# Rounding the last chunk's intermediate rows in two halves, and placing unread TensorE products by the planner's own clock

## The chip, the core and the metric

The kernel runs on one core of one Trainium2 chip. A core has five engines that work side by side, each through its own instructions in order: TensorE (PE in the profile; PEld is its loading of weights), VectorE (DVE), ScalarE (ACT), GpSimd (POOL) and SyncE (SP), which here issues the transfers between memory and the on-chip buffers. The metric is the time of one execution on the device in microseconds (us). The kernel before takes 2631.14 us, the median of three runs (2631.13 to 2632.89).

## What is computed

The input `x` has 8 sequences of 1024 rows and 256 columns, in 32 bit. Four blocks follow each other, each added to its own input:

```
x = x + linear_attention_layer(layernorm(x))    # 16 heads of 16, running sums over the rows,
                                                # then norm, 256->1024 gelu ->256, norm
x = x + relu(layernorm(x) @ w1 + b1) @ w2 + b2  # 256->1024->256
x = x + softmax(Q K^T / 16) V                   # of layernorm(x), one head of 256
x = x + fp4_linear(silu(g) * u, w_down)         # g, u = fp4_linear(layernorm(x), w_gate / w_up)
```

The last block has 704 intermediate columns. `fp4_linear` rounds both of its operands, in blocks of 16 neighbouring columns, to a grid of eight sizes times a scale that is the block's largest size over 6. A block of 16 is rounded without looking at any other block, and 352 columns are 22 whole blocks.

## The kernel before, in words

**Tiling.** Rows are taken in chunks of 128 (8 in a sequence, 64 in all) and, in the first two blocks, in groups of 4 chunks (16 groups). A product on TensorE has 128 rows of weights and up to 512 columns; its result lies in one of 8 banks of PSUM. 32 bit products appear in the trace as two records, turns (transposes) as one.

**The stages.** `linear_group` and `linear_span` (lines 909 to 1125) make a group's normalized rows (`n`, `n0T`), its `k` and `q` (products of `n0T` with `wk` and `wq`), and a serial chain of running sums: sums on DVE (`prod`), a product with `hsum` on PE, a reciprocal and a product (`flow`) on DVE, spreading over the rows, sums again (`hsum` a second time), an exponential on ACT (`e`), a small product (`total,front`), and `scale`. The first group is cut into two spans, chunks 0 and 1 and chunks 2 and 3, and spreads `flow` and `scale` by products with `mask`; all other groups spread them through memory (two `packed` writes, then `spread` reads, on SP). `linear_chunk` (1127) does the attention of one chunk (`qz`, `sc`, `v_pad`, `kv_sum`, `wo`) and ends in `h`. `dense` (1331) makes the two wide blocks from halves of a group, with `w_in` and `w_out` streamed from memory through five buffers each; `norms_1` (1441) and `norms_2` (1462) stand behind its halves. `soft_chunk` (1502) makes softmax and the fp4 block of one chunk. The fp4 weights (`w_raw`) are rounded once, in the first 345 us, by `fp4_weights` (691).

**The end of a chunk.** `soft_chunk` makes `hid` (128 x 704) in two column halves: two products each for gate and up, `Silu` on ACT, a product on DVE. Then `fp4` (650) rounds all 704 columns at once: largest size, scale and reciprocal on DVE, a scaling, a square on ACT (`q_c`), four more DVE instructions. PE turns `hid` in six tiles, four into one bank and two into another; ACT copies each bank (`hqT`); six products with `wdT` give the row block, DVE adds `rows` to it (`y`), and SP writes it out.

**Who sets the order.** The order of all instructions is fixed when the kernel is built. Every stage is a Python generator that yields what its next step needs: an engine, tiles, banks, a condition (`when`) and a place in the order (`at`). `Plan.run` (291) always goes on with the part that can start first by the planner's own model of time. The model is in `Plan.took` (160): each call that is recorded by `Queue` (324, all its instructions carry line 337 in the profile) is given a start and a cost, and moves `free`, the time from which its engine is free, `done`, the time at which a tile is written, and `ran`, the time at which TensorE's last product ends. A product that starts over 2 us behind `ran` sets `slow`: up to then, products are costed at twice their length.

**Unread products.** Where the plan sees TensorE standing for more than 1.6 us ahead of its next step, `run` calls `fill` (1650), which puts in products of the identity matrix with itself, whose result nobody reads:

```
pause = max(now, best[2]) - self.ran
if pause > 1.6 and ...:
        self.fill(pause - 0.7)
```

`fill` takes 0.22 off that length for each product. The products go through `took` like all others, from `free["tensor"]` on, which may lie behind `ran`; `run` then sets `free` anew. `ident` is made by a helper outside the plan, so the plan has no time for it.

Of the kernel before, what the change touches and what calls it, by code (L numbers as in the profile page):

```python
# [22 lines left out]
INTER = 704  # L23
# [12 lines left out]
INTER_TILES = [(t * P, min(P, INTER - t * P)) for t in range((INTER + P - 1) // P)]  # L36
# [26 lines left out]
class Plan:  # L63
# [11 lines left out]

    def __init__(self, tc, nc):
        self.tc, self.nc = tc, nc
        self.free = {}
        self.done = {}
        self.by = {}  # L80
        self.banks = []
        self.live = {}
        self.slots = {}
        self.kind = {}
        self.size = {k: v[0] for k, v in TILES.items()}
        self.spare = False
        self.used = {}
        self.held = set()
        self.kept = set()
        self.last = {}  # L90
        self.act_set = 0
        self.landed = [0.0] * 8
        self.tiled = False
        self.ran = self.slow = 0.0
        self.fill = None
        self.parts = []
        for name in ("tensor", "vector", "scalar", "gpsimd", "sync"):
            setattr(self, name, Queue(self, name))
# [157 lines left out]
    def pe(self, *tiles, **kw):  # L256
        return self.need("tensor", tiles, **kw)

    def dve(self, *tiles, **kw):
        return self.need("vector", tiles, **kw)  # L260

    def act(self, *tiles, **kw):
        return self.need("scalar", tiles, **kw)
# [27 lines left out]
    def run(self):  # L291
        while self.parts:
            now = self.free.get("tensor", 0.0)
            best = None
            for part in self.parts:
                t = self.ready(part[1])
                if t is None:
                    continue
                stays = self.tiled and part[1].tiled
                queue = part[1].queue  # L300
                wait = max(max(t) - now - (0.3 if stays or part[2] < 0.0 else 0.0), 0.0)
                urgent = part[2] < 0.0
                unripe = 0.0 if urgent else max(t[1] + self.RIPE[queue] - now, 0.0)
                key = wait, unripe, queue == "tensor", not stays, part[2]
                if best is None or key < best[0]:
                    best = key, part, max(t)
            assert best is not None, "every part waits for another"
            pause = max(now, best[2]) - self.ran
            if pause > 1.6 and best[1][1].queue == "tensor" and self.fill is not None:
                if (self.banks_free(best[1][1].banks + 1) or 0.0) <= self.ran + 0.4:  # L310
                    self.fill(pause - 0.7)
            if best[0][0] > 0.0 or best[1][1].queue == "tensor":
                self.free["tensor"] = max(now, best[2])
            part = best[1]
            need = next(part[0], None)
            if need is None:
                self.parts.remove(part)
            else:
                part[1] = need
                if need.at is not None:  # L320
                    part[2] = need.at
# [34 lines left out]
def block_stack_kernel(ctx: ExitStack, tc: tile.TileContext, a: dict, out: bass.AP):  # L356
# [20 lines left out]
    plan = Plan(tc, tc.nc)  # L377
    nc, pe, dve, act, dma = plan, plan.pe, plan.dve, plan.act, plan.dma
    x_dram = a["L0_attn_inputs"]
    B, L, _ = x_dram.shape  # L380
    NCH = L // P
# [20 lines left out]
    def fresh(kind, need, name=None):  # L402

        need.fresh = kind
        yield need
        return make(kind, name)
# [49 lines left out]
    nc.gpsimd.iota(row_i, pattern=[[0, 1]], base=0, channel_multiplier=1)  # L456
    ident = const.tile([P, P], F32, name="ident")
    make_identity(tc.nc, ident)
    bdiag = const.tile([P, P], F32, name="bdiag")
    make_block_diagonal(tc.nc, bdiag, DH)  # L460
    triu = const.tile([P, P], F32, name="triu")
# [188 lines left out]
    def fp4(src, width, rows=P):  # L650

        nb = width // QB
        src = src[:rows, :width]  # L660
        amax = small([P, INTER // QB], "x_amax", 2)[:rows, :nb]
        nc.vector.tensor_reduce(
            amax, blocks(src, width), AX.X, ALU.max, apply_absolute_value=True
        )
        sc = small([P, INTER // QB], "x_s", 4)[:rows, :nb]
        nc.vector.tensor_scalar(sc, amax, 1.0 / 6.0, 1e-12, ALU.mult, ALU.max)
        rc = small([P, INTER // QB], "x_r", 3)[:rows, :nb]
        nc.vector.reciprocal(rc, sc)
        yield dve(rc)
        nc.vector.scalar_tensor_tensor(  # L670
            blocks(src, width),
            blocks(src, width),
            1.0 - 2.0**-23,
            wide(rc, rows, nb),
            ALU.mult,
            ALU.mult,
        )
        tile_c = yield from fresh("q_c", act(src))
        c = tile_c[:rows, :width]
        nc.scalar.activation(c, src, AF.Square, scale=(2.0**22 / 6.0) ** 0.5)  # L680
        yield dve(c)
        nc.vector.tensor_scalar(c, c, 2.0**22 * 4.0 / 3.0, None, ALU.add)
        nc.vector.tensor_tensor(src, src, c, ALU.add)
        yield dve(src)
        nc.vector.tensor_tensor(src, src, c, ALU.subtract)
        plan.drop(tile_c)
        nc.vector.tensor_tensor(
            blocks(src, width), blocks(src, width), wide(sc, rows, nb), ALU.mult
        )
# [812 lines left out]
    def soft_chunk(cc):  # L1502
# [2 lines left out]
        q = seqs[s]  # L1505
        n2T, vt = q["n2T"], q["vt"]
        at = 3.5 + min(cc, B * NCH - 10) / 4
        yield pe(
            banks=1,
            when=lambda: count["asked"] == cc  # L1510
            and count["asked"] - count["valued"] < (3 if plan.spare else 2),
        )
        bank = mm_bank()
        for e in range(2):
            for k in range(2):
                nc.tensor.matmul(
                    bank[:, e * P : (e + 1) * P],
                    lhsT=wqk[:, k, e * P : (e + 1) * P],
# [10 lines left out]
        banks = []  # L1529
        for kb in range(NG):  # L1530
            yield pe(qT, banks=1)
            bank = mm_bank()
            plan.keep(bank)
            for e in range(2):
                nc.tensor.matmul(
                    bank, lhsT=qT[:, e, :], rhs=n2T[kb][:, e, :], start=e == 0, stop=e == 1
# [9 lines left out]
        prob = []  # L1546
# [9 lines left out]
        for kb in range(NG):  # L1556
            yield pe(prob[kb], banks=1, at=at + 0.25)
            bank = turned([prob[kb][:, j * P : (j + 1) * P] for j in range(G)])
# [32 lines left out]
        for j0 in range(0, INTER, INTER // 2):  # L1591
            cols = slice(j0, j0 + INTER // 2)
            yield pe(xqT, banks=2)
            gb, ub = mm_bank()[:, : INTER // 2], mm_bank()[:, : INTER // 2]
            for bank, wT in ((gb, wgT), (ub, wuT)):
                for k in range(2):
                    nc.tensor.matmul(
                        bank,
                        lhsT=xqT[:, k, :],
                        rhs=wT[:, k, cols],  # L1600
                        start=k == 0,
                        stop=k == 1,
                    )
            if hid is None:
                hid = yield from fresh("hid", act(gb))
            else:
                yield act(gb)
            nc.scalar.activation(hid[:, cols], gb, AF.Silu)
            yield dve(hid)
            nc.vector.tensor_tensor(hid[:, cols], hid[:, cols], ub, ALU.mult)  # L1610
        plan.drop(xqT)
        yield dve(hid)
        yield from fp4(hid, INTER)
        hqT = []
        for half in range(2):
            yield pe(hid, banks=1, at=at + 0.75)
            tiles = INTER_TILES[4 * half : 4 * half + 4]
            bank = turned([hid[:, f0 : f0 + P] for f0, _ in tiles])
            hqT.append((yield from fresh("prob", act(bank), "hqT")))
            hqT[half] = hqT[half].rearrange("p (k t) -> p k t", k=4)  # L1620
            nc.scalar.copy(hqT[half][:, : len(tiles), :], bank)
        yield pe(*hqT, banks=1)
        bank = mm_bank()
        for k in range(len(INTER_TILES)):
            nc.tensor.matmul(
                bank[:, :D],
                lhsT=hqT[k // 4][:, k % 4, :],
                rhs=wdT[:, k, :],
                start=k == 0,
                stop=k == len(INTER_TILES) - 1,  # L1630
            )
# [6 lines left out]
        nc.sync.dma_start(out=out[s, c * P : (c + 1) * P, :], in_=y)  # L1638
        plan.drop(y)

    def softmax_and_fp4():
        for cc in range(B * NCH):
            q = seqs[cc // NCH]
            yield dve(
                at=3.5 + min(cc, B * NCH - 10) / 4,
                when=lambda: q["normed"] == NCH and cc - count["out"] < (8 if plan.spare else 4) and "softmax" in weights and "ends" in late,
            )
            plan.start(soft_chunk(cc), 3.5 + min(cc, B * NCH - 10) / 4)

    def fill(us):  # L1650

        bank = mm_bank()
        while us > 0.0:
            nc.tensor.matmul(bank[:, :P], lhsT=ident, rhs=ident, start=True, stop=True)
            us -= 0.22
        plan.let_go(bank)

    plan.fill = fill
# [45 lines left out]
```

## Time and profile before

| | |
|---|---|
| median of three runs | 2631.14 us |
| profiled execution | 2630.5 us |
| its span (first to last instruction) | 2628.6 us |
| PE busy | 2595.1 us |
| DVE busy | 1924.2 us |
| ACT busy | 1297.4 us |
| unread products (`bank<-ident`) | 94 products, 188 records, 24.0 us busy |
| first record on PE | 3.10 us |
| last product on PE starts, DVE's last `y` | 2622.56 us, 2625.45 us |

Times are counted from the first instruction. A row of the order of time has its start, its length, the engine, the line, the operation, output and inputs by their names in the program, shapes, the number of merged records, and in brackets the idle time of the engine ahead of it with what ended it. A row of busy time by stage has the stretch, its length, busy us (and records) of the engines in the order PE, PEld, DVE, ACT, POOL, then the granted clock of TensorE as a share of full speed, the busy share of the transfer engines and GB/s; where it was asked for one engine, it has that engine's busy time alone. A row of a group has the operation with its shapes and count, then busy us and mean ns of one, then idle time ahead of it with what ended it.

### The profile page before, as it was taken

How to read it: one execution, taken by the hardware profiler on the slowest of the kernel's cores; microseconds unless marked ns; L12 is line 12 of the kernel's file. 1: busy time of each engine (PE TensorE's matmuls, PEld its weight loads, DVE VectorE, ACT ScalarE, POOL GpSimd, SP SyncE). 2: the span in 40 equal slices, each digit the busy share in tenths (PEclk: the TensorE clock that was granted, in tenths of full speed). 3: DMA queues.
4: the chain of work that ended last, by engine and by line, in shares of the span. 5: the costliest groups of instructions: out<-in, count | busy, mean ns of one | idle time of the engine just before them, and what ended most of it. 6: DMA issues, size and time to landing. Idle time of an engine off the chain costs nothing.

```text
span 2628.6 us, 46432 instructions
## 1 busy us (share of the span) xinstructions
PE 2595.1 (99%) x16891; PEld 2031.8 (77%) x16891; DVE 1924.2 (73%) x4353; ACT 1297.4 (49%) x2665; POOL 577.7 (22%) x1101
## 2 busy tenths in 40 slices
PE   8989999999999999999999999999999999999999
PEld 7777777777777777787777777777787777877777
DVE  7888786868768587685867768686785877755687
ACT  4534445455364554636445364553645545354443
POOL 2333232222212122131221312122121221211000
PEclk9999999999999999999999999999999999999999
DMA  3425333223132232322323223232322312222000
GB/s 94 125 86 155 99 87 103 79 69 107 57 99 73 71 109 62 91 71 76 101 65 98 68 82 85 74 105 63 93 75 69 109 59 87 71 77 81 25 3 22
DMA packets 286819, 211.94 MB, mean 81 GB/s; under 512 B 24704, under 2 KB 275072, under 8 KB 286592
## 3 DMA queue, kind: packets, MB, share of 16 engines
q1 hardware_dynamic: 286592, 208.97, 27.7%
q8 instruction: 135, 2.21, 0.3%
q14 instruction: 92, 0.75, 0.1%
HBM read 188.17 MB, written 20.71 MB: 79 GB/s over the span
## 4 chain that ended last, share of the span: by engine, by line
PE 86%; DVE 8%; DMA 2%; ACT 2%; issue 1%; POOL 0%; SPq 0%; DVEq 0%; POOLq 0%; ACTq 0%
PE bank L337 86%; DVE prod L337 3%; DMA spread<-packed 2%; ACT L337 1%; DVE spread L337 1%; DMA packed<-flow 1%; DVE ln_st L337 0%; DVE u L337 0%; ACT prob L337 0%; DVE hid L337 0%; DVE r L337 0%; DVE res L337 0%; DVE w_raw L337 0%; ACT n0T L337 0%; DVE ln_mv L337 0%
## 5 line engine op out<-in xcount | busy, mean ns | idle before, releaser
L337 PE MATMUL bank<-half,w_in 128*128 128x256 f32 x2048 | 530.5, 382 | 3.6 <-DVE res L337 1.2
L337 PE MATMUL bank<-w_out,hidden 128*128 128x256 f32 x2048 | 532.2, 383 | 0.2 <-ACT hidden L337 0.2
L337 POOL TENSOR_SCALAR ln_ve<-ln_mv 128x1 f32<-128x1 f32 x384 | 97.7, 254 | 1691.8 <-DVE ln_mv L337 1672.4
L337 PEld LDWEIGHTS bank<-w_out,hidden 128*128 128x128 f32 x2048 | 369.5, 190 | 92.7 <-issue 39.7
L337 PEld LDWEIGHTS bank<-half,w_in 128*128 128x128 f32 x2048 | 380.2, 191 | 76.7 <-issue 26.6
L337 ACT ACT_TABLE_LOAD x322 | 413.1, 1283 | 7.9 <-DVE nmax L337 2.0
L337 ACT ACTIVATE hidden<-bank,c_L_ffn_b 128x256 f32<-128x256 f32 x256 | 121.7, 475 | 333.7 <-PE bank L337 333.6
L337 POOL TENSOR_TENSOR ln_rstd<-ln_ve,neghalf 128x1 f32<-128x1 f32 x384 | 238.0, 620 | 32.0
L337 PE MATMUL bank<-n2T,qT 128*128 128x512 f32 x512 | 241.7, 594 | 0.2 <-ACT qT L337 0.2
L337 PE MATMUL bank<-vt,probT 128*128 128x256 f32 x1024 | 231.5, 379 | 0.0
L337 PEld LDWEIGHTS bank<-vt,probT 128*128 128x128 f32 x1024 | 193.4, 190 | 28.3 <-issue 2.4
L337 ACT ACTIVATE hidden<-bank,c_L_attn_b 128x256 f32<-128x256 f32 x256 | 120.2, 470 | 187.0 <-PE bank L337 186.8
L337 PE MATMUL bank<-wdT,hqT 128*128 128x256 f32 x768 | 176.2, 379 | 0.5 <-ACT hqT L337 0.5
L337 PE MATMUL bank<-wgT,xqT 128*128 128x352 f32 x512 | 172.5, 459 | 0.0
L337 PE MATMUL bank<-wuT,xqT 128*128 128x352 f32 x512 | 172.3, 459 | 0.0
L337 DVE TENSOR_TENSOR hid<-hid,bank 128x352 f32<-128x352 f32 x116 | 59.9, 516 | 151.8 <-PE bank L337 124.2
L337 PEld LDWEIGHTS bank<-wdT,hqT 128*128 128x128 f32 x768 | 145.3, 190 | 20.9 <-ACT hqT L337 0.7
L337 DVE TENSOR_TENSOR sc<-bank,triu 128x512 f32<-128x512 f32 x240 | 148.7, 680 | 8.4 <-PE bank L337 7.7
L337 PEld LDWEIGHTS bank<-n2T,qT 128*128 128x128 f32 x512 | 92.8, 190 | 66.9 <-issue 59.8
L337 PEld LDWEIGHTS bank<-wuT,xqT 128*128 128x128 f32 x512 | 97.3, 190 | 54.2
L337 PEld LDWEIGHTS bank<-wgT,xqT 128*128 128x128 f32 x512 | 94.2, 190 | 32.9 <-issue 0.7
L337 DVE TENSOR_REDUCE mx<-bank 128x1 f32<-128x512 f32 x128 | 86.2, 674 | 35.0 <-PE bank L337 35.0
(220 smaller groups left out, 4401.6 us busy)
## 6 DMA issues: line engine op xcount, KB each, us to landing
w_in<-in_L_attn_W_dram SPq DMA_DIRECT2D x256, 128.0 KB
w_out<-in_L_attn_W_dram SPq DMA_DIRECT2D x256, 128.0 KB
w_in<-in_L_ffn_w_dram SPq DMA_DIRECT2D x256, 128.0 KB
w_out<-in_L_ffn_w_dram SPq DMA_DIRECT2D x256, 128.0 KB
spread<-packed SPq DMA_DIRECT2D x90, 256.0 KB
x<-in_L_attn_inputs_dram SPq DMA_DIRECT2D x64, 128.0 KB
xr<-in_L_attn_inputs_dram SPq DMA_DIRECT2D x64, 128.0 KB
rows<-res SPq DMA_DIRECT2D x64, 128.0 KB
```

What stands on the lines that cost most here:

```text
L337: ins = method(*args, **kw)
```

## The change

There are two edits.

In the planner, `fill` is no longer given a length but the time up to which products are wanted: 0.8 ahead of the step that TensorE waits for. It puts `free["tensor"]` back to `ran`, lets `took` place the products one by one, at the lengths that `took` gives them (twice as long while the model holds TensorE's clock to be slow), until that time is reached, and then restores `free`. The plan also knows from now on that `ident` is written by POOL at 3.0, and `free["tensor"]` begins at 0.0 explicitly. The order of all other instructions follows from the planner's model, in which `ran` and `slow` now differ.

In `soft_chunk`, the last chunk of all (`alone`) starts a part `half_rounded` for each column half of `hid` as soon as it is made, which rounds 352 columns by itself. PE then turns two tiles (columns 0 to 255, out of the first half) into the first bank and four into the second, ACT copies the banks, and the first two products with `wdT` need the first copy alone. All other chunks are as before.

```diff
@@ -75,7 +75,7 @@
 
     def __init__(self, tc, nc):
         self.tc, self.nc = tc, nc
-        self.free = {}
+        self.free = {"tensor": 0.0}
         self.done = {}
         self.by = {}
         self.banks = []
@@ -308,7 +308,7 @@
             pause = max(now, best[2]) - self.ran
             if pause > 1.6 and best[1][1].queue == "tensor" and self.fill is not None:
                 if (self.banks_free(best[1][1].banks + 1) or 0.0) <= self.ran + 0.4:
-                    self.fill(pause - 0.7)
+                    self.fill(max(now, best[2]) - 0.8)
             if best[0][0] > 0.0 or best[1][1].queue == "tensor":
                 self.free["tensor"] = max(now, best[2])
             part = best[1]
@@ -456,6 +456,7 @@
     nc.gpsimd.iota(row_i, pattern=[[0, 1]], base=0, channel_multiplier=1)
     ident = const.tile([P, P], F32, name="ident")
     make_identity(tc.nc, ident)
+    plan.done[ident.tensor.name], plan.by[ident.tensor.name] = 3.0, "gpsimd"
     bdiag = const.tile([P, P], F32, name="bdiag")
     make_block_diagonal(tc.nc, bdiag, DH)
     triu = const.tile([P, P], F32, name="triu")
@@ -1505,6 +1506,7 @@
         q = seqs[s]
         n2T, vt = q["n2T"], q["vt"]
         at = 3.5 + min(cc, B * NCH - 10) / 4
+        alone, rounded = cc >= B * NCH - 1, []
         yield pe(
             banks=1,
             when=lambda: count["asked"] == cc
@@ -1608,23 +1610,31 @@
             nc.scalar.activation(hid[:, cols], gb, AF.Silu)
             yield dve(hid)
             nc.vector.tensor_tensor(hid[:, cols], hid[:, cols], ub, ALU.mult)
+            if alone:
+                plan.start(half_rounded(hid, cols, rounded), at + 0.6)
         plan.drop(xqT)
-        yield dve(hid)
-        yield from fp4(hid, INTER)
+        if not alone:
+            yield dve(hid)
+            yield from fp4(hid, INTER)
         hqT = []
-        for half in range(2):
-            yield pe(hid, banks=1, at=at + 0.75)
-            tiles = INTER_TILES[4 * half : 4 * half + 4]
+
+        cut = 2 if alone else 4
+        for first, tiles in ((0, INTER_TILES[:cut]), (cut, INTER_TILES[cut:])):
+            yield pe(
+                hid, banks=1, at=at + 0.75, when=lambda: not alone or len(rounded) > bool(first)
+            )
             bank = turned([hid[:, f0 : f0 + P] for f0, _ in tiles])
-            hqT.append((yield from fresh("prob", act(bank), "hqT")))
-            hqT[half] = hqT[half].rearrange("p (k t) -> p k t", k=4)
-            nc.scalar.copy(hqT[half][:, : len(tiles), :], bank)
-        yield pe(*hqT, banks=1)
+            t = (yield from fresh("prob", act(bank), "hqT")).rearrange("p (k t) -> p k t", k=4)
+            nc.scalar.copy(t[:, : len(tiles), :], bank)
+            hqT.append(t)
+        yield pe(*(hqT[:1] if alone else hqT), banks=1)
         bank = mm_bank()
         for k in range(len(INTER_TILES)):
+            if alone and k == cut:
+                yield pe(hqT[1])
             nc.tensor.matmul(
                 bank[:, :D],
-                lhsT=hqT[k // 4][:, k % 4, :],
+                lhsT=hqT[k // cut if k < cut else 1][:, k % cut if k < cut else k - cut, :],
                 rhs=wdT[:, k, :],
                 start=k == 0,
                 stop=k == len(INTER_TILES) - 1,
@@ -1638,6 +1648,13 @@
         nc.sync.dma_start(out=out[s, c * P : (c + 1) * P, :], in_=y)
         plan.drop(y)
 
+    def half_rounded(hid, cols, rounded):
+
+
+        yield dve(hid)
+        yield from fp4(hid[:, cols], INTER // 2)
+        rounded.append(cols)
+
     def softmax_and_fp4():
         for cc in range(B * NCH):
             q = seqs[cc // NCH]
@@ -1647,12 +1664,13 @@
             )
             plan.start(soft_chunk(cc), 3.5 + min(cc, B * NCH - 10) / 4)
 
-    def fill(us):
+    def fill(until):
 
         bank = mm_bank()
-        while us > 0.0:
+        now, plan.free["tensor"] = plan.free["tensor"], plan.ran
+        while plan.free["tensor"] < until:
             nc.tensor.matmul(bank[:, :P], lhsT=ident, rhs=ident, start=True, stop=True)
-            us -= 0.22
+        plan.free["tensor"] = now
         plan.let_go(bank)
 
     plan.fill = fill
```

## The prediction

> **What bounds the kernel now.** I read the page first, then busy time by stage, then the order of events where TensorE is not full. Span and shares:
>
> ```profile
> span 2628.6 us, 46432 instructions
> ...
> PE 2595.1 (99%) x16891; PEld 2031.8 (77%) x16891; DVE 1924.2 (73%) x4353; ACT 1297.4 (49%) x2665; POOL 577.7 (22%) x1101
> ```
>
> PE is the bound, so the end moves only by what PE loses: idle time, products that nobody reads (they count as busy), and time at half clock. Busy time by stage (window, length, then each engine, granted clock, DMA share, GB/s):
>
> ```profile
> 0.00:60.31 60.31, 51.13 (x480) 43.88 (x480) 42.87 (x113) 23.99 (x64) 13.63 (x38) 1.00 0.37 97
> 60.31:161.41 101.10, 92.39 (x627) 72.84 (x627) 82.08 (x200) 47.24 (x118) 28.89 (x53) 0.97 0.40 114
> 161.41:340.00 178.59, 174.50 (x1419) 137.75 (x1420) 144.92 (x328) 84.48 (x197) 58.11 (x103) 1.00 0.41 116
> 340.00:605.00 265.00, 262.56 (x1760) 206.22 (x1759) 190.02 (x431) 132.46 (x268) 64.51 (x119) 1.00 0.29 83
> 605.00:2620.00 2015.00, 2009.59 (x12587) 1567.26 (x12586) 1462.60 (x3283) 1008.37 (x2017) 412.55 (x790) 1.00 0.26 75
> ```
>
> PE idles 9.2 us before 60.31, 8.7 in the next 101, 6.5 up to 605 and 5.4 in the 2015 us after that. What nobody reads, by shape:
>
> ```profile
> L337 PE MATMUL bank<-ident 128*128 128x128 f32 x188 | 24.0, 290 | 3.1 <-POOL ident masks.py:199 3.1
> ```
>
> That is 94 products of two records each, all before 137 us. The first 31 stand ahead of the first real work (order of time):
>
> ```profile
> 3.10 9.02 PE L337 MATMUL bank<-ident 128*128 128x128 f32 x62 [3.10 <-POOL ident masks.py:199]
> ...
> 6.58 0.41 DVE L337 TENSOR_SCALAR n<-x,ln_mv,ln_rstd 128x256 f32<-128x256 f32 x1
> ...
> 7.54 0.41 DVE L337 TENSOR_SCALAR n<-x,ln_mv,ln_rstd 128x256 f32<-128x256 f32 x1
> ...
> 11.96 0.60 PE L337 MATMUL bank<-ident,n 128*128 128x128 f32 x4
> ```
>
> The rows n are complete at 6.99 and 7.95, and PE turns them at 11.96, after the last of the 31. Last, the clock in the stall around 140 us (PE busy, granted clock):
>
> ```profile
> 140.09:143.50 3.41, 0.88 (x4) 1.00 0.11 38
> 143.50:146.92 3.42, 2.86 (x10) 0.50 0.01 2
> 146.92:150.33 3.41, 3.41 (x10) 0.50 0.13 38
> ```
>
> After 3.41 us with PE 26% busy the clock is at half for 6.8 us; the 6.3 us of work in it (from 144.06 on) take 3.1 us longer than at full.
>
> **The change part by part.** In the built order of the changed kernel all PE work is that of before, except for the unread products: 13, 7, 20, 12, 5, 4, 8, 17 (86) where before has 31, 7, 20, 12, 16, 8 (94). The order differs up to the place that before reaches at 605 us and is the same from there on. A warm product costs 0.23 us (40 records in 4.63, less overlap). I walked the new order by the durations of before, and count what PE loses.
>
> *First 13 products.* Their 26 records are 18 in the 3.87 us at half clock (3.10 to 6.97) and 8 at 0.11: they end at 7.9, the second n is ready at 7.95, so the turns start at 8.0, 4.0 us earlier. The first product with wk follows 1.12 us behind the turns (11.96 to 13.08), at 9.1. DVE gives part of it back: its constants run until 11.04 and two rows' statistics until 11.7, so the first running sum moves from 14.75 to 11.7, and the statistics of row 3, now behind it, push the second to 12.9 (15.62 before). The products k*prod, which before waited for ACT until 17.51, start at 13.95. Kept: 3.5 us. Does wk arrive by 9.1? No row before 13.08 shows it. It is issued third, at 1.70, and some 700 KB have moved by 5.0 (96 GB/s to 3.10, then 209); I take it as there (ends: nothing lost, or all 4.0 if it lands at 13.08).
>
> *The 16 products at 54.83 go, and the sums of rows 2 and 3 move behind the first chunk* (hsum from 44.90 to behind v_pad,k; mask, from 47.60, behind the second chunk's wo). In before's own time: v_pad,k of chunk 0 at 46.65 in place of 47.34, wo 48.0 for 49.58, second v_pad,k 50.55 for 52.20. Then DVE stands: h waits for POOL's rstd until 51.3 (0.7 us, with kv, the reciprocal and flow queued behind it), flow ends at 53.45, mask runs 53.6 to 55.6, h of row 1 ends at 56.95, its turn is at 57.0 and the first w_in at 57.9 for 60.31. Gain 2.4; lead here 5.9.
>
> *From there to before's 161.41.* Before loses 8.7 idle, 1.9 in 8 products and 3.1 at half clock: 13.7. The new order loses, by the walk: 5 and 4 products, 2.1; two wo behind ACT copies that queue after eight score activations, 1.0; the second hidden behind one more pair of table loads (1.28 each), 1.5; hsum of group 1 behind DVE, 0.5; the late w_in of before (128.17), 0.65. Then the stall of group 1. DVE reaches its first running sum at 99.8 for 104.16 and flow at 111.3 for 116.77; the two packed writes and four spread reads on SP have 4 issues between them for 6, and land 7.0 us behind flow, as the second group does in before (151.31 to 158.35). DVE has only 3.6 us of work for that time, then 12.9 us of sums: the second hsum runs 131.3 to 132.3 for before's 137.06 to 139.25, after a wait of 0.6. Behind it n of the other half is ready at 134.2 (wait 1.9), 8 products (1.85), front at 138.3 behind Exp and its table load (wait 2.1), 17 products (3.85) to 142.6, while scale is ready at 141.65. Sum 16.1, so 2.4 more than before: lead 3.5.
>
> In that sum the clock stays full. I bound it by rows: at 26% busy it fell, and with 2.03 of 3.41 us (136.68 to 140.09, 59%) it stayed; the new stall has some 1.3 of 3.41 (38%), between them. Falling costs half of 6.8 us, 3.4; I take 0, because the 25 products come just there, and keep both ends.
>
> [...] In this trace no gap of that stall is over 1.6 us, and the clock fell. [...]
>
> *161 to 605.* Before idles 6.5 us. One wait can be followed: front at 242.50 waits 1.3 us behind 1.73 us of PE work after hsum; the new order puts 3.7 us there. I take half of that 1.2, because others are new and cannot be followed: 0.6 (ends: 2.4 lost, as at 531 to 569, or 3.2 gained, half of all).
>
> *The last chunk's halves.* The end of before (order of time):
>
> ```profile
> 2619.94 0.89 DVE L337 TENSOR_TENSOR hid<-hid,x_s 128x704 f32<-128x704 f32 x1
> 2621.28 0.82 PE L337 MATMUL bank<-ident,hid 128*128 128x128 f32 x6
> ...
> 2621.92 0.86 ACT L337 COPY hqT<-bank 128x512 f32<-128x512 f32 x2 [2.60 <-PE bank L337]
> ...
> 2622.56 2.86 PE L337 MATMUL bank<-wdT,hqT 128*128 128x256 f32 x12 [0.46 <-ACT hqT L337]
> 2625.45 0.42 DVE L337 TENSOR_TENSOR y<-bank,rows 128x256 f32<-128x256 f32 x1 [3.54 <-PE bank L337]
> ```
>
> Rounding ends at 2620.83, before PE is free (2621.28); only 0.46 us of PE waits for the copy. Now eight DVE instructions of 704 columns (5.4 us) become sixteen of 352 (between the 256 and 704 rows: 2 x 3.3 = 6.6), and ACT's second Square stands behind the copy of the chunk before it (2618.95 to 2619.32). The first half is ready at 2618.9, the second at 2621.9, 1.0 later than now. PE turns two tiles at 2621.3, four at 2621.95, then multiplies the first two while the other copy (0.59) runs: end of products 2625.36 for 2625.42. Gain 0.1 (ends: 0.46 gained if the second half is in time, 0.7 lost if it is 1 us later still).
>
> Sum: 3.5 + 0.6 + 0.1 = 4.2. The profiled execution took 2630.5 (span 2628.6 and 1.9 around it), and the median of the runs is 0.6 above it: 2626.3 and 0.6, 2626.9.
>
> **The rivals.** About 0.2% (5.3 us) is what a measurement of this kernel can tell from no change: faster is below 2625.9, slower above 2636.4.
> *Faster: the products only fill waits.* If the 17 end with scale (0.95) and the walk's waits for wo, hidden and hsum (3.0) don't come, 2622.9. For it: before has none of these three waits over 0.3. Against: the moved copies and table loads are in the built order. Chance 0.40.
> *The clock falls in the stall of group 1*: 2626.9 + 3.4 = 2630.3. For it 38% against 59%, against it the 25 products. Chance 0.12.
> *Slower: DVE becomes the bound of the first groups.* It is 82.1 of 101.1 us busy from 60 to 161 and nearly full from 120 to 144. The new order leaves it standing 0.7 for rstd, 1.6 behind ACT's table loads at 98 and 3.4 for the spread reads: 5.7, which eats the lead of 5.9; then 34 products past 60 us for 8 (26 x 0.23 = 5.9) are lost in full: 2631.1 - 5.9 + 5.7 + 5.9 = 2636.8. It decides if the second hsum of group 1 starts no earlier than 137. Against: DVE's work ahead of it is smaller by a weight piece (2.8 us). Chance 0.10.
>
> **How the numbers follow.** The likeliest case (0.38; its own range 2625.9 to 2630) and the clock's (0.12) lie within 0.2%: 0.50. Faster 0.40, slower 0.10. The low end is the faster rival with 3.2 more from 161 to 605, 2619.7; the high end is the clock's case with the tail's 0.7 and 2.4 lost before 605, 2633.4; so 2619.5 to 2634.
>
> **What would show it.** First turns of n at 8.0 and wk's product at 9.1; first w_in at 54.4 (60.31 now); group 1's second hsum near 131, its front near 138, scale at 142.6; clock 1.00 from 130 to 160; 172 records of unread products; the last chunk's second half complete some 0.4 us after PE ends the product before it. It is wrong if the first wk product stays near 13, if the clock falls in the stall, or if PE idles more than 16 us between the first w_in and the first qz,k of group 1.

## The result, and the profile after

The changed kernel takes 2635.18 us (median of 20 runs, 2632.74 to 2637.73) against 2631.18 (20 runs, 2629.33 to 2633.80): a ratio of 1.0014, with a 95% interval of 1.0007 to 1.0020. It is 4.0 us slower, within the 0.2% that the prediction called no change, but on the other side of zero from the forecast (2626.9) and above its range (2619.5 to 2634). The profiled execution took 2633.7; span and shares from its page:

```profile
span 2632.0 us, 46414 instructions
...
PE 2597.0 (99%) x16875; PEld 2032.5 (77%) x16875; DVE 1920.6 (73%) x4361; ACT 1294.0 (49%) x2661; POOL 573.4 (22%) x1101
```

The unread products are the 172 records of the built order, 86 products:

```profile
L337 PE MATMUL bank<-ident 128*128 128x128 f32 x172 | 22.8, 294 | 3.1 <-POOL ident masks.py:199 3.1
```

For the stages, the two kernels are cut where both have done the same set of real products: the first w_in (56.19, before 60.31), a product at 203.92 (203.03) and the place where the orders meet again (604.92, before 601.60). Columns as in the table of before: window, length, busy time of PE, PEld, DVE, ACT and POOL, granted clock, DMA share, GB/s. Before, cut there:

```profile
0.00:60.31 60.31, 51.13 (x480) 43.88 (x480) 42.87 (x113) 23.99 (x64) 13.63 (x38) 1.00 0.37 97
60.31:203.03 142.72, 133.43 (x1062) 104.04 (x1063) 114.73 (x278) 69.27 (x165) 44.25 (x82) 0.98 0.35 102
203.03:601.60 398.57, 392.62 (x2733) 310.86 (x2731) 299.26 (x673) 193.46 (x416) 107.26 (x193) 1.00 0.35 99
601.60:2620.00 2018.40, 2012.99 (x12597) 1569.16 (x12596) 1465.63 (x3288) 1009.82 (x2020) 412.55 (x790) 1.00 0.26 75
```

The changed kernel:

```profile
0.00:56.19 56.19, 45.47 (x412) 37.04 (x412) 40.57 (x107) 23.84 (x62) 14.40 (x39) 0.96 0.41 104
56.19:203.92 147.73, 139.35 (x1114) 109.93 (x1115) 113.03 (x273) 68.99 (x164) 42.31 (x80) 0.97 0.34 98
203.92:604.92 401.00, 394.35 (x2733) 311.25 (x2732) 299.73 (x685) 189.62 (x413) 104.14 (x193) 1.00 0.34 98
604.92:2623.40 2018.48, 2012.59 (x12595) 1570.35 (x12594) 1464.67 (x3292) 1010.55 (x2022) 412.51 (x790) 1.00 0.26 75
```

The first row ends 4.1 us earlier than before; the second takes 5.0 longer and the third 2.4 longer. Look at the clock: 0.96 and 0.97 in the first two rows, where before has 1.00 and 0.98. Before fell once, at 143.50. The changed kernel keeps its clock there and loses it in three other places. Windows of 3.41 us around them:

```profile
14.24:17.65 3.41, 1.38 (x9) 0.88 (x9) 3.15 (x7) 1.03 (x4) 2.03 (x3) 1.00 0.27 78
17.65:21.06 3.41, 3.41 (x21) 2.09 (x20) 0.39 (x2) 0.47 (x1) 0.00 (x0) 0.50 0.87 250
51.78:55.20 3.42, 2.05 (x17) 1.86 (x18) 3.10 (x8) 0.19 (x1) 0.82 (x3) 1.00 0.00 0
55.20:58.61 3.41, 2.95 (x9) 2.09 (x10) 3.08 (x7) 2.36 (x5) 1.21 (x5) 0.50 0.00 0
89.33:92.74 3.41, 1.50 (x8) 0.96 (x6) 2.64 (x6) 1.32 (x4) 3.03 (x6) 1.00 0.01 2
92.74:96.16 3.42, 1.64 (x10) 1.34 (x14) 3.32 (x8) 0.46 (x2) 1.49 (x2) 0.50 0.18 54
96.16:99.57 3.41, 3.41 (x67) 2.83 (x61) 0.39 (x3) 0.93 (x3) 2.12 (x4) 0.50 0.27 86
...
140.53:143.94 3.41, 1.70 (x39) 1.38 (x32) 3.24 (x12) 0.31 (x1) 2.44 (x6) 1.00 0.29 83
```

PE was busy for 1.38, 2.05 and 1.50 us of the window ahead of each fall. The work done at half clock (3.41, 2.95, 1.64 and 3.41 us) would take about half of that time at full clock, so an estimate of the loss is 5.7 us (the first product with a `w_in`, four records, takes 2.08 us here and 1.13 in before), where before lost 3.1 by the same count (2.86 and 3.41 us of work). How the first of these windows came about is seen in PE's order of time:

```profile
8.14 0.60 PE L337 MATMUL bank<-ident,n 128*128 128x128 f32 x4
9.26 1.13 PE L337 MATMUL bank<-n0T,wk 128*128 128x256 f32 x4 [0.52 <-ACT n0T L337]
...
16.14 0.44 PE L337 MATMUL bank<-ident,n 128*128 128x128 f32 x2 [1.38 <-DVE n L337]
17.23 1.70 PE L337 MATMUL bank<-n0T,wk 128*128 128x256 f32 x4 [0.66 <-ACT n0T L337]
```

The same turn and product in before:

```profile
19.24 0.44 PE L337 MATMUL bank<-ident,n 128*128 128x128 f32 x2 [0.66 <-DVE n L337]
20.33 1.13 PE L337 MATMUL bank<-n0T,wk 128*128 128x256 f32 x4 [0.66 <-ACT n0T L337]
```

The first turns start 3.8 us earlier, as the change intended. Then PE catches up with VectorE, whose constants are as late as before, and waits 1.38 and 0.66 where before waited 0.66 and 0.66. That is 0.7 more of waiting. The wk product behind it runs mostly at half clock and takes 1.70 where before took 1.13.

### The profile page after: what moved, and what is told of

Its sections match the earlier page's. It is cut to its first block, busy times and chain, and to the rows that moved or that the text cites. A ratio compares the mean times of both kernels' runs of the same rounds, so it can differ in the third digit from the quotient of the medians.

```text
span 2632.0 us, 46414 instructions
## 1 busy us (share of the span) xinstructions
PE 2597.0 (99%) x16875; PEld 2032.5 (77%) x16875; DVE 1920.6 (73%) x4361; ACT 1294.0 (49%) x2661; POOL 573.4 (22%) x1101
## 4 chain that ended last, share of the span: by engine, by line
PE 85%; DVE 9%; DMA 3%; ACT 2%; issue 1%; POOL 1%; SPq 0%; DVEq 0%; ACTq 0%; POOLq 0%
PE bank L337 85%; DVE prod L337 3%; DMA spread<-packed 2%; ACT L337 1%; DVE spread L337 1%; DMA packed<-flow 1%; DVE ln_st L337 1%; DVE n L337 0%; DVE u L337 0%; DVE w_raw L337 0%; ACT prob L337 0%; DVE r L337 0%; POOL ln_rstd L337 0%; DMA packed<-scale 0%; DVE ln_mv L337 0%
```

## The experiments

All ratios are to the kernel before, run beside each version on the same chip, with 95% intervals. The median of before was 2631.18 beside the changed kernel, 2632.24 beside e1 to e4, 2631.87 beside e5 to e8 and 2630.65 beside e9 to e11. So medians of different groups differ by up to 1.6 us for no reason of the kernel's, and are best compared by their ratios.

| run | median us | ratio | interval |
|---|---|---|---|
| changed kernel | 2635.18 | 1.0014 | 1.0007 to 1.0020 |
| e1, halves alone | 2631.07 | 0.9996 | 0.9986 to 1.0005 |
| e2, planner alone | 2635.22 | 1.0014 | 1.0005 to 1.0022 |
| e3, changed, gaps filled | 2631.59 | 0.9996 | 0.9987 to 1.0005 |
| e4, before, 13 first | 2629.90 | 0.9992 | 0.9983 to 1.0001 |
| e5, before, 13 first, gaps filled | 2625.70 | 0.9977 | 0.9968 to 0.9986 |
| e6, before, stall filled | 2628.86 | 0.9990 | 0.9981 to 0.9998 |
| e7, changed, stall bare | 2638.69 | 1.0024 | 1.0015 to 1.0033 |
| e8, changed, waits filled from 0.8 us | 2634.08 | 1.0009 | 1.0000 to 1.0018 |
| e9, as e5, w_in's wait filled, halves | 2623.88 | 0.9971 | 0.9960 to 0.9983 |
| e10, changed, 32 first | 2638.11 | 1.0026 | 1.0015 to 1.0036 |
| e11, changed, first gap filled | 2633.67 | 1.0012 | 1.0003 to 1.0020 |

Two theories stood against each other. The *clock theory*: the loss is work at half clock, and products that nobody reads are worth their place where they keep the clock up. The *waits theory*: VectorE sets the pace of the first groups, slow products only fill waits for it, and what matters is the order.

**e1 and e2: which half of the change.** e1 gives before the new `soft_chunk` and `half_rounded`; e2 takes them out of the changed kernel again.

> The kernel before with only the last chunk's rows rounded in halves; planner and order as before. Both theories (clock, waits) say nothing of this part. In the changed kernel the stretch from the first of the last two wdT products to the end of the last is 6.36 us, in before 6.73, so -0.4 us of 2631.2, nothing that can be told from no change: 2630.8. If the tail alone brought the slowdown: 2635.

> The changed kernel with the last chunk as before: only the planner's part. If the loss lies in the first groups (both theories), 2635.2 + 0.4 = 2635.6, slower than before by 0.17%; with the clock at half for three stretches before 100 us, as in the changed kernel. If it lay in the tail, 2631.

Both came as expected: 2631.07 and 2635.22. All of the measurable slowdown belongs to the planner's part. What the halves are worth (0.4 by the trace) lies inside e1's interval. The profiled execution of e2 has falls at 18.82, 56.36 and 93.91, as expected, and one more at 1117.91.

**e3: the same order, with the gaps filled.** Products are issued into the bank that the next real work is about to overwrite, and the plan does not count them, so that nothing else moves: every other engine's order is that of the changed kernel.

```diff
+EXTRA = {10: 5, 11: 2, 40: 4, 42: 2, 44: 5, 45: 1, 85: 6, 87: 9}
...
-            plan.took(self.name, op, args, kw)
+            plan.unseen or plan.took(self.name, op, args, kw)
...
     def mm_bank():
         bank = ps.tile([P, 512], F32, tag="bank", name="bank")
         plan.bank(bank)
+        plan.nth += 1
+        plan.unseen = True
+        for _ in range(EXTRA.get(plan.nth, 0)):
+            nc.tensor.matmul(bank[:, :P], lhsT=ident, rhs=ident, start=True, stop=True)
+        plan.unseen = False
         return bank
```

> The changed kernel, same order on every engine, with 34 more unread products put where TensorE waits ahead of the three falls of its clock (5 and 2 at 14.8 to 17.2 us, 4, 2, 5 and 1 at 48.7 to 56.2, 6 and 9 at 89.5 to 94.5), unseen by the plan. Clock theory: no fall before 110 us; 5.7 us of half clock on real work goes, products that outlast their wait cost some 0.5: 2635.2 - 5.2 = 2630, first w_in near 53.3 (56.19 now). Waits theory (VectorE is late, and slow products only fill waits for it): clock at 1.00 but the lead at the first row of n of the second group no better, 2635 or, with the products in the way, 2636.

2631.59: with 34 products more the kernel is 3.6 us faster than e2, the planner's part alone, on the same chip, and by the ratios 0.18% (4.7 us) faster than the changed one. Busy time and clock to the first w_in and on to 160 us:

```profile
0.00:54.30 54.30, 47.87 (x449) 40.18 (x449) 40.12 (x107) 23.85 (x62) 14.13 (x36) 1.00 0.43 108
54.30:160.00 105.70, 100.08 (x726) 80.68 (x728) 86.72 (x212) 49.37 (x123) 31.32 (x63) 1.00 0.38 109
```

The clock is 1.00 throughout, and the first w_in starts at 54.46 (56.19 in the changed kernel). At the turns of group 1 (162.7 us) its profiled execution is 4.8 us ahead of the changed kernel's, and by the end 4.2: the half clock was on the path. The orders of the real work are the same on every engine, so no order stands behind this gain. It misses the expected 2630 by 1.6, inside its interval. It does not come near the forecast, so something else costs time too.

**e11: one gap alone.** Only `EXTRA = {10: 5, 11: 2}`.

> The changed kernel with 5 and 2 more unread products in the first gap alone (n and n0T, 14.8 to 17.2 us). Clock theory: the fall at 17.65 goes, those near 55 and 92 stay: 1.6 us, 2633.6. Waits theory: 2635.2.

2633.67, where the clock theory put it, but before was 0.5 us faster beside it, and the interval (2631.4 to 2635.9) holds both theories. In its trace the fall at 17.65 is gone, and those at 55.50 and 93.05 are there. The trace decides for the clock: 1.45 us of lead over the changed kernel behind the gap, 1.5 still at 203 us. Behind that this execution loses 3.7 us against the changed kernel's in the same order and with no further fall (near 795 us it waits 1.51 for a running sum, the changed kernel 0.67). So single executions drift by a few us in the later part, and only leads taken near a gap say what the gap is worth.

**e7: the opposite.** The changed kernel keeps its clock in the stall of the second group, where the forecast saw 4 in 10 of a window busy. Take its 25 products away:

```diff
+        plan.batches = getattr(plan, "batches", 0) + 1
         while plan.free["tensor"] < until:
-            nc.tensor.matmul(bank[:, :P], lhsT=ident, rhs=ident, start=True, stop=True)
+            if plan.batches in (7, 8):
+                plan.took("tensor", "matmul", (bank[:, :P],), dict(lhsT=ident, rhs=ident))
+            else:
+                nc.tensor.matmul(bank[:, :P], lhsT=ident, rhs=ident, start=True, stop=True)
```

> The changed kernel without the 8 and 17 unread products in the stall of the second group (the plan still counts them). Clock theory: the window that was 50% busy comes to some 35%, the clock falls near 144 and stays low for one or two windows with 3.4 to 5 us of work in them at double time after the scale: 2635.2 + 2.5 = 2637.7 (from 2637 to 2639). If products in a wait only cost: 0.4 earlier (they end 0.36 behind the scale), 2634.8.

2638.69, slower than the changed kernel by 3.5 us in the medians and by 0.10% (2.6 us) in the ratios, whose intervals overlap, for 25 products fewer. The windows of that stall:

```profile
143.94:147.35 3.41, 0.44 (x2) 0.20 (x2) 3.22 (x10) 1.76 (x3) 1.80 (x3) 1.00 0.27 89
147.35:157.59 10.24, 6.76 (x19) 5.56 (x20) 8.55 (x25) 1.60 (x6) 3.54 (x7) 0.50 0.15 43
```

A window 13% busy, and then three at half clock, with 6.76 us of work in them: 3.4 us lost by half of the work. Against the changed kernel's execution it is 1.8 us behind at 132 us and 3.8 behind at 160, so the stall costs 2.0 net, near the 2.5 expected. The 1.8 ahead of it have another source: the clock fell at 51.77 for three windows, where the changed kernel's fell at 55.20 for one, although the two programs are the same up to there and their grids lie within 0.01 us of each other. The window ahead of 51.77 was 51% busy in both; one kept the clock and one lost it.

**e6: before, with its own stall filled.** `EXTRA = {124: 6, 125: 4, 126: 3}` on the kernel before.

> The kernel before with 13 more unread products in the stall of the second group alone (6, 4 and 3 ahead of w_raw, n and front, 139.7 to 144). Clock theory: the fall at 143.5 goes and with it the 3.1 us that work loses at half clock: 2628.4. Waits theory: the scale that ends this stall comes from VectorE, so nothing moves: 2631.5.

2628.86. The windows that were 26% busy and at 0.50 before:

```profile
140.00:144.00 4.00, 3.63 (x33) 3.25 (x30) 3.79 (x14) 1.87 (x4) 3.50 (x8) 1.00 0.19 66
144.00:151.00 7.00, 6.78 (x38) 5.88 (x38) 6.09 (x18) 3.65 (x12) 0.23 (x1) 1.00 0.17 48
```

Its profiled execution is 0.7 behind before's ahead of the stall (132 us of before) and 2.3 in front where before has its clock back (150.64): 3.0 gained, 3.1 expected. VectorE's scale came no earlier (it starts at 147.99, in before at 147.69), so the gain is not VectorE's. The waits theory, which had this stall end by that scale in any case, falls here.

**e4, e5 and e9: the short first batch in the old order.** e4 issues 13 of the first 31 products of before, with the plan unaware of it:

```diff
+        issued, first = 0, plan.ran == 0.0
         while us > 0.0:
-            nc.tensor.matmul(bank[:, :P], lhsT=ident, rhs=ident, start=True, stop=True)
+            if first and issued >= 13:
+                plan.took("tensor", "matmul", (bank[:, :P],), dict(lhsT=ident, rhs=ident))
+            else:
+                nc.tensor.matmul(bank[:, :P], lhsT=ident, rhs=ident, start=True, stop=True)
+            issued += 1
             us -= 0.22
```

> The kernel before, same order, with 13 of its first 31 unread products issued (the plan still counts 31). Turns of n at 8.0 for 11.96. Clock theory: the waits that come into the open behind it (n and n0T at 14 to 17.5 us) make the clock fall there as in the changed kernel and cost 0.7 of wait and 1.4 to 1.7 of half clock: 4.0 - 2.3 = 1.7 kept, first w_in at 58.6, 2629.5, with the fall at 143.5 as before. If no fall comes: 3.3 kept, 2627.9. Waits theory (VectorE's constants set the pace): nothing kept at the first w_in, 60.3, 2631.

2629.90. Of 3.9 us at the first turns, 1.25 are left at 22.7, because the clock falls as in the changed kernel (e5, which keeps it there, has 3.3 left); and it stays low for longer in the stall of the second group:

```profile
13.99:17.40 3.41, 1.19 (x8) 0.65 (x7) 3.15 (x7) 1.11 (x5) 2.46 (x3) 1.00 0.17 44
17.40:20.81 3.41, 3.27 (x16) 2.29 (x18) 0.73 (x2) 0.56 (x2) 0.11 (x1) 0.50 0.83 224
136.87:140.28 3.41, 1.40 (x34) 0.80 (x26) 3.31 (x11) 0.37 (x1) 1.59 (x4) 1.00 0.22 71
140.28:150.52 10.24, 8.28 (x25) 6.30 (x26) 7.30 (x22) 4.05 (x11) 2.29 (x5) 0.50 0.08 26
```

e5 adds `EXTRA = {10: 6, 11: 2, 42: 3, 124: 6, 125: 3, 126: 3}`.

> The kernel before in its order with 13 of its first 31 unread products, and 23 more where TensorE then waits: 6 and 2 ahead of n and n0T (14.7 to 17.5 us), 3 ahead of h (51.5), 6, 3 and 3 in the stall of the second group (139 to 144). Clock theory: no fall at all; 2.9 us of lead from the start, cut to some 0.7 where w_in lands at 127.7 whatever the lead, then 3.1 of half clock saved at 143.5: 2631.5 - 0.7 - 3.1 = 2627.7, faster than both kernels. Waits theory (slow products only fill waits): 2630 as with 13 alone.

2625.70, 2 us better than expected and 0.23% faster than before. The lead at 132 us is 0.3, as small as expected; up to 150.64 of before the stall gives 4.7 in place of 3.1, because its waits shrink too (idle from 132 to 149 us: 0.7, before 4.5). And that although the clock fell once, in a place that was not filled:

```profile
123.33:126.74 3.41, 1.39 (x7) 0.88 (x6) 3.34 (x4) 0.47 (x1) 0.14 (x1) 1.00 1.10 274
126.74:130.16 3.42, 3.42 (x10) 2.66 (x9) 3.27 (x7) 0.47 (x1) 0.00 (x0) 0.50 0.55 168
```

PE is early here and waits 2.02 us for the transfer of a w_in. e9 puts 8 products ahead of that w_in (`118: 8`) and takes the halves as well.

> The run with 13 first products and the gaps filled, in the order of before, with 8 more products ahead of the w_in that lands late (124 to 126.2, where the clock fell at 126.74), and with the last chunk in halves. Clock theory: that fall goes too, 1.7 us of half clock, but the second group's sums that follow are paced by VectorE in part, so 1.0 to 1.7; halves 0.4: 2625.7 - 1.7 = 2624.0. If products in a wait for a transfer only cost: 2626.

2623.88, against 2624.0 expected. No fall is left:

```profile
0.00:60.00 60.00, 52.51 (x489) 44.31 (x490) 45.83 (x119) 26.66 (x69) 14.86 (x39) 1.00 0.40 99
60.00:160.00 100.00, 95.26 (x677) 76.61 (x676) 83.98 (x206) 47.18 (x119) 31.87 (x57) 1.00 0.41 117
```

This is the fastest of the versions: 0.29% faster than before (0.17 to 0.40%).

**e8: let the planner fill shorter waits.** In the changed kernel, `if pause > 0.8` in place of `if pause > 1.6`.

> The changed kernel with the planner filling waits from 0.8 us on in place of 1.6: 3 and 1 products in the first gap (n, n0T), 4 between mask and h, 2 ahead of k, 2 ahead of wo and some later; one turn of n moves behind h. Clock theory: the falls at 17.65 and 55.2 go (2.0 and 1.5 us of loss), the one at 92.7 stays: 2632. Waits theory: 2635.

2634.08, where 2632 was expected, and only 1.1 us better than the changed kernel (1.3 by the ratios). The three early falls are all gone, the third too; but one turn of n moved behind a turn of h, n waited 1.24 and 1.78 us near 254 and 356, and a late running sum at 795 brought a fall at 796.70. How much of the miss belongs to each wasn't separated.

**e10: the long first batch in the new order.** One line of the change is left out:

```diff
-    plan.done[ident.tensor.name], plan.by[ident.tensor.name] = 3.0, "gpsimd"
```

> The changed kernel without the line that tells the plan when ident is done: 32 first products for 13, all else and every order the same. Clock theory: the first turns 4.2 us later, the two waits at 14.8 to 17.2 us shorter by 0.7 and no fall at 17.65 (1.7 saved): 1.8 later, 2637.0, with the later falls as before. If the first batch is worth its full length: 2639.4. If VectorE sets the pace of the first chunk: 2635.2.

2638.11, 2.9 us behind the changed kernel (3.2 by the ratios), 1.1 more than expected and inside the interval; its profiled execution has one fall more, at 798.85, behind a late running sum. Its order is that of the changed kernel, which waits 0.67 for that sum and not 2.01, so this fall belongs to the execution and not to the version. In the trace the first turns come 4.0 later, and 2.2 of it are left at 26.6, since the fall at 17.65 doesn't come. The short first batch is a gain in either order; the fall behind it takes back almost half.

## Why the prediction was wrong

**Two of its steps failed.** The first is the clock. "In that sum the clock stays full" was argued for one place, the stall of group 1, and there it was right, if narrowly: 1.70 us of the 3.41 were busy (50%; 38% estimated), and the clock stayed, while in e7 a window at 51% lost it. But the steps "first 13 products" and "the 16 products at 54.83 go" opened three other windows, and none of them was held against the rows that the forecast had itself put up (26% fell, 59% stayed). The waits in the first were known to the walk; what they do to the work behind them was left out. So the sum has 0 where the trace has 5.7 us, of which e3 got back 4.8 by 203 us. With the clock held, e3 stands at that place 3.9 us ahead of before (203.03 to 199.10), where the sum had a lead of 3.5 at 161; the changed kernel stands 0.9 behind.

The second is "161 to 605: 0.6 gained". The orders can't be cut at the same work between 141 and 203 us; from there to 605 the trace lost 2.4 (398.57 us before, 401.00 after), at the edge of the bounds given. It isn't the clock: e3 is as far ahead of the changed kernel at 567 us (4.9) as at 165 (4.8), so it loses the same. The wait of 1.3 us for front that the forecast followed did go. In its place PE waits four times for an n, 3.1 us in all (3.3 in e3), where before and e9, in the old order, never wait for one. One place can be seen. In before, VectorE in order of time:

```profile
252.50 0.41 DVE L337 TENSOR_SCALAR n<-res,ln_mv,ln_rstd 128x256 f32<-128x256 f32 x1
...
253.90 1.49 DVE L337 TENSOR_TENSOR q<-q,spread 128x512 f32<-128x512 f32 x2
```

In the changed kernel the same n stands behind the two products with the spread reads, and these wait for their transfers:

```profile
254.24 0.69 DVE L337 TENSOR_TENSOR q<-q,spread 128x512 f32<-128x512 f32 x1 [1.35 <-DMA spread<-packed]
255.45 0.69 DVE L337 TENSOR_TENSOR q<-q,spread 128x512 f32<-128x512 f32 x1 [0.52 <-DMA spread<-packed]
256.06 0.41 DVE L337 TENSOR_SCALAR n<-res,ln_mv,ln_rstd 128x256 f32<-128x256 f32 x1
```

PE then waits 0.78 for that n. The slower rival had VectorE standing for spread reads as well, in the stall of group 1; here it does so where the forecast didn't look. Of the 2.4, PE's idle time as a whole is only 0.7. The other 1.7 are in busy time, with as many records as before: they cover more time between them, turns of n above all (1.6 us of it). What lies behind that was not followed up, and that this one position in VectorE's order explains the whole loss was not tried.

What the new order costs as a whole can be read from e9 and e3 up to the place where the orders meet again, 601.60 in before: both have the short first batch and a full clock up to there, and differ in order and in unread products (107 and 120). e9 gets there at 595.54 and e3 at 599.99, the changed kernel at 604.92. So from before to e9 is 6.1 gained, the new order with its products gives back 4.4, and the falls of the clock 4.9 more. Thirteen products more, at 0.22 us (eight in a row took 1.78 in e9), can be up to 2.9 of the 4.4 where they outlast a wait; this was not separated.

**By its other steps:**
- First turns at 8.0, first wk product at 9.1: 8.14 and 9.26. wk had landed. "Kept: 3.5": 1.67 at 42.8 us of the changed kernel, and 3.1 with the 1.45 that e11 gets back by holding the clock there.
- "Gain 2.4" to the first w_in: 2.45. The w_in came at 56.19 for 54.4; with the clock held (e3) it came at 54.46.
- "Sum 16.1" of waits and products in the next stage: 8.4 idle (147.73 less 139.35, none of it behind 163.1) and, at 0.23 each, 7.8 in 34 products from 56.19 to 203.92: 16.2. That sum is right in part by luck, since its split is not that of the walk (one wo waited 1.45, one n 2.25 at 94.5); and 3.7 at half clock stand beside it.
- The stall of group 1: front waited 1.03 for 2.1, the 17 products ended 0.36 behind the scale for 0.95. The fall priced as a rival didn't come. But the stall stood later than the walk put it: the second hsum at 140.35 for 131.3, and still at 135.9 in e3. VectorE's pace up to it was not that of the walk. The slower rival was to decide if that hsum started no earlier than 137; so it did, and its 2636.8 is near the result, but with the clock held the condition isn't met, so that nearness is luck.
- The tail: from the start of the last but one wdT product to the end of the last 6.36 us, 6.73 before, so 0.37 gained for 0.1 forecast. The second half is complete when PE needs it:

```profile
2624.82 0.52 DVE L337 TENSOR_TENSOR hid<-hid,x_s 128x352 f32<-128x352 f32 x1
2624.95 1.10 PE L337 MATMUL bank<-ident,hid 128*128 128x128 f32 x6
...
2625.89 2.83 PE L337 MATMUL bank<-wdT,hqT 128*128 128x256 f32 x12
```

The wait of 0.46 ahead of the last products is gone.

None of the three signs that the forecast named for its own failure came: wk wasn't late, the stall kept its clock, PE idled 8.4 us and not 16. The forecast watched one stall for a danger that came true in three other places. Long waits did not mark them: no wait over 1.5 us ended in the window ahead of any of the changed kernel's three falls (at the third, a wait of 2.25 us had run for 0.46), while the stall of group 1, which kept its clock, has one of 1.72.

## What to carry to other kernels

Before taking filler work from the bounding engine, or moving work ahead of its inputs, go through the whole stretch in windows of 3.41 us, the length measured here, and ask of each how busy the engine will be; here waits of 1.38 and 0.66 us cost 1.45 us more in the work behind them. Filler is free only as long as it ends with the wait (the first 31 products of before held its first turns 4.0 us past the second n), and in these runs it was worth having where a fall stood behind a window that was 26% busy without it (e6) or 40, 60 and 44% (e3). And where a planner orders the work, a small edit to its clock is a new order: test the edit's effect in the old order, with the plan left unaware, before believing that it is the edit that gains or loses.

## What the runs showed of the chip

- In these profiles the granted clock changed on a grid of 3.41 us that ran on through the execution: in the changed kernel at 7.41, 17.65, 21.06, 55.20, 58.61, 92.74 and 99.57, all multiples of 3.413 apart to 0.02. Its place against the kernel differed from run to run (first full clock at 6.0 to 8.6 us in 13 profiled kernels); that this place alone decides whether a stall falls or holds was not shown. Waits differed too: for the running sum near 795 us, PE waited 0.59 to 2.02 us in the seven profiles with the new planner, and the clock fell behind it in the two with over 2.0.
- In these 13 profiles the clock fell 22 times before the end. The grid window ahead was 13 to 48% busy in 20 of them; 51 and 60% in the others. Of some 9,900 windows that kept the clock, two were under 49% (44 and 48%). The window at 60% is the one in which 1.94 of 2.05 busy us went to flow,mask products over 64 of the 128 rows. The one at 51%, in e7, has a twin in the changed kernel that kept the clock at 51%. What set these two falls apart was not shown.
- Windows full of turns (ident,n and the like) kept the clock: near 2570 to 2585 us, five of the profiles have a window that is 97% busy with them and 37% without, and the clock stayed, while six windows that were 41 to 57% busy without turns lost it.
